# A graph network whose GpSimd gathers wait for TensorE: earlier TensorE steps for the attention's first chunks, and a last early chunk gathered in two halves

## The chip, the cores and the metric

The kernel runs on one core of one Trainium2 chip. The core has five engines with a queue of instructions each: TensorE (PE in the profile; its weight loads are PEld), VectorE (DVE), ScalarE (ACT), GpSimd (POOL) and SyncE (SP, which issues loads and stores here). 16 DMA engines move data between HBM and the core's memory. The metric is the time of one execution on the device, in microseconds (us); the figure for a kernel is the median of its timed runs.

## The reference: what is computed

One layer norm, then a graph network of two convolutions and one attention over 6250 nodes of 128 features and 200000 edges. The edges are sorted by their target node `dst`; `src` is random.

```python
h = max(layernorm(x), 0)
for (w1, b1, g, bt, w2, b2) in two convolutions:
    m   = concat(h[dst], h[src], edge_attr) @ w1 + b1
    m   = silu(group_norm(m, g, bt)) @ w2 + b2
    h   = segment_sum(m, dst) / count          # then a node's norm, silu, a residual
q, k, v = h @ qw + qb, h @ kw + kb, h @ vw + vb          # 8 heads of 16
logits  = (q[dst] * k[src]).sum(-1) * 16 ** -0.5 + edge_attr @ ew + eb
pe      = exp(logits - segment_max(logits, dst)[dst])
o       = segment_sum(pe / segment_sum(pe, dst)[dst] * v[src], dst)
out     = x + h + group_norm(o @ ow + ob)
```

## The kernel before

**Tiles and stages.** The nodes are cut into 49 tiles of 128. The edges are cut into 1563 columns of 128, and eight columns make a chunk (`TPC = 8`), so there are 196 chunks (`NCH`); chunk number `c` counts from the last edges backwards, and the last chunk, 195, has three columns. Three pipelines run over all chunks one after the other: convolution 1, convolution 2, attention. Between two of them the work of node tile 0 ends a layer (`last_tile`, lines 1188 to 1205): it can start only when the last chunk's sums are there.

**What an edge needs.** What comes from `dst` is read by SyncE as a window of consecutive rows (`pk`, from table `a_d`) and spread over the edges by a matmul with a one-hot matrix `ohT`, which ScalarE makes from a row of indices `rel` (lines 763 and 764; SyncE loads `rel` for two chunks at a time, line 725). What comes from `src` is gathered by GpSimd, a column at a time: line 796 is one indirect DMA of 128 rows, eight of them to a chunk (table `b_d` in the convolutions, `kv_d` in the attention). Besides 35 small one-hot instructions at the very end (line 1673) GpSimd does nothing else in the pipelines.

**Early chunks.** The next pipeline's first three chunks (`EARLY = 3`) are gathered before node tile 0 is done, from copies of the tables that lack it (`b_e`, `kv_e`). Tile 0's share, `late`, is then added by a matmul with a one-hot matrix `ohS` (line 1252 in convolution 2, `complete` with line 1700 in the attention). Chunk 3 is the first that is gathered from the whole table.

**Order.** The instructions of DVE, SP, ACT and PE stand in the order in which the program writes them, and each gather follows the gather before. Step `n` of `pipeline` (lines 893 to 957) issues the loads and the gathers of chunk `n + 2` (`ahead = 2`), then writes the work of chunk `n` and the products of chunk `n + 1`. In the attention a chunk's work is: `products` (line 1521, TensorE, into the one buffer `qe`), the product with the gathered keys (line 1536, DVE), a copy of the edge terms (line 1538, ACT; it frees `qe`), the head sums (line 1540). Chunks are collected in runs (chunks 0 to 3, then 4 to 11, then eight at a time); when a run is full its maxima are found (lines 1569 and 1570), and only then its chunks are weighted (line 1595, DVE), which frees their gather buffers, and summed (line 1602). The attention has 11 gather buffers (`ge0` to `ge2`, `g3` to `g9`, `gl`), the convolutions have four.

**The hold.** A gather waits for its buffer. Beside that, the first gather of a chunk is held until TensorE has come to a certain instruction:

```python
kept.seen = last_product() if fetched else None        # line 917, in pipeline, ahead of stage.fetch
if t == 0 and kept.seen is not None:                   # line 804, in gather
    held(h, kept.seen)
```

`last_product()` (line 810) is the TensorE instruction that was written last. In step `n` of the attention it is the end of the products of chunk `n`. The first chunk whose loads a pipeline issues inside its steps is not held (`fetched`): chunk 2 in convolution 1, chunk 3 in convolution 2, which finds its first three gathered, and chunk 2 in the attention, whose gathers are done by then, so that there chunk 3 is held. The early chunks, which the pipeline ahead gathers, are held in the same way (line 921); for chunk 2 of them this adds no wait, because GpSimd has waited for that TensorE instruction by then.

Of the kernel before, what the change touches and what calls it, by code (L numbers as in the profile page):

```python
# [31 lines left out]
TPC = 8  # L32
# [6 lines left out]
EARLY = 3  # L39
# [18 lines left out]
def kernel(ctx: ExitStack, tc: tile.TileContext, x, src, dst, eat, w, out):  # L58
# [12 lines left out]
    NCH = -(-EI // TPC)  # L71
# [16 lines left out]
    kept = SimpleNamespace(h0=hpc.tile([P, NW, D], FP, name="h0"))  # L88
# [80 lines left out]
    b_d = {i: dram.tile([NW * P, D], FP, name=f"b_d{i}") for i in (1, 2)}  # L169
    kv_d = dram.tile([NW * P, KV], FP, name="kv_d")  # L170
    b_e = dram.tile([NW * P, D], FP, name="b_e")
    kv_e = dram.tile([NW * P, KV], FP, name="kv_e")
# [72 lines left out]
    with tc.tile_pool(name="node0", bufs=1) as np_, tc.tile_pool(name="prep", bufs=1) as pp, \  # L245
# [99 lines left out]
        back, firsts = sums[:, :NCH], sums[:, 2 * P:2 * P + NCH]  # L345
# [445 lines left out]
            tc.add_to_no_dep_group(key, h.ins)  # L791

    def gather(k, g, table_d, ring=None):
        n = k.nt
        for t in range(n):
            h = nc.gpsimd.indirect_dma_start(  # L796
                out=g[:, t, :table_d.shape[1]], out_offset=None, in_=table_d,
                in_offset=bass.IndirectOffsetOnAxis(ap=k.src[:, t:t + 1], axis=0))
            if ring is None:
                continue  # L800
            if kept.behind is not None:
                follows(h, kept.behind)
            kept.behind = h.ins
            if t == 0 and kept.seen is not None:
                held(h, kept.seen)
            ring.mark(h, k.at, t, n - 1)

    kept.behind = kept.seen = None

    def last_product():  # L810
        return next((i.name for i in reversed(nc.cur_bb.bb.instructions) if i.engine == mybir.EngineType.PE), None)

    def held(h, name):
        tc.add_manual_dep(
            h.ins, name, mybir.DependencyInfo(mybir.DependencyClass.Sync, mybir.DependencyReason.DATA),
            reason="held until TensorE is there")
# [76 lines left out]
    def pipeline(i, stage, following=None, aside=iter(()), then=iter(())):  # L893


        ends, todo = steps_of(i)
        starts = {n: j for j, (n, _, _) in enumerate(plans[i])}
        ahead = stage.ahead
        ks, under_way, said, fetched = stage.ks, [], {}, False

        def go_on(n, those):
            for g in those:
                if said.get(g) == "held" and n + 1 in ends:
                    continue
                said[g] = next(g, STOP)
                if said[g] is STOP:
                    under_way.remove(g)

        for c in range(ahead):
            if c not in ks:  # L910
                ks[c] = stage.fetch(c)
                compared(ks[c])
        stage.products(ks[0])
        for n, seconds in enumerate(todo):
            new = None
            if n + ahead < NCH and n + ahead not in ks:
                kept.seen = last_product() if fetched else None
                new = ks[n + ahead] = stage.fetch(n + ahead)
                kept.seen, fetched = None, True
            elif following and n + ahead >= NCH:  # L920
                kept.seen = last_product()
                new = following.prefetch(n + ahead - NCH)
                kept.seen = None
            if n + 1 < NCH and stage.soon:
                stage.products(ks[n + 1])
            run = [ks[c] for c in ends.get(n, ())]
            stage.root(run)
            early = stage.soon and n > NCH - SOON
            if early:
                ahead_of = [g for g in under_way if said.get(g) not in ("var", "root")]  # L930
                go_on(n, ahead_of)
            if new and stage.soon:
                compared(new)
            first = (lambda k: lambda: stage.first(k))(ks[n]) if n < NCH else None
            stage.then = [ks[c] for c in (todo[n + 1] if n + 1 < len(todo) else ()) if c in ks]
            if stage.second(run, [ks.pop(c) for c in seconds], first) and first:
                first()
            stage.finish()
            if new and not stage.soon:
                compared(new)  # L940
            if n + 1 < NCH and not stage.soon:
                stage.products(ks[n + 1])
            if n + 1 < len(todo):
                stage.early(ks, n, todo[n + 1])
            if n in starts:
                for _ in aside:
                    pass
                under_way.append(stage.batch(starts[n]))
            go_on(n, [g for g in under_way if not early or g not in ahead_of])
            if n > 4 and next(aside, STOP) is STOP and n > min(starts):  # L950
                next(then, None)
            if n < NCH:
                stage.reduce(ks[n])
        stage.flush()
        for g in (*under_way, aside, then):
            for _ in g:
                pass
# [206 lines left out]
    def nodes_of(b, i, w, m, hx=None):  # L1164
        return attention_nodes(b, w, m, hx) if i == 3 else conv_nodes(b, i, w, m, last=hx is not None)
# [22 lines left out]
    def last_tile(b, i, hx=True):  # L1188

        slots, b.bank = b.bank(), None  # L1190
        turn = itertools.cycle(range(BN))

        def slot():
            j = next(turn)
            return slots[:, j:j + 1, :]

        b.bank = slot
        b.var = lambda: last_var
        b.rs = last_rs
        nc.scalar.activation(last_sd[:, :1], eps_t, AF.Sqrt)  # L1200
        for r in nodes_of(b, i, 0, 1, hx):
            if r == "root":
                nc.scalar.activation(last_sd, last_var, AF.Sqrt, bias=eps_t, scale=1.0 / HD)  # L1203
            if r == ("inverse" if i == 3 else "root"):
                nc.vector.reciprocal(last_rs, last_sd)  # L1205
# [10 lines left out]
    def convs(general=False):  # L1216
        with ExitStack() as es:
            pool = lambda n, b, **kw: es.enter_context(tc.tile_pool(name=f"{n}{'g' if general else 'c'}", bufs=b, **kw))
            pools = {"oh": pool("oh", 2), "ps": pool("ps", 1, space=PSUM)}
            if not general:  # L1220
                pools["ohT"] = pool("ohT", 2)
                ring = Ring("ring", GB)
# [75 lines left out]

            class Stage:
                ahead, soon = 2, True  # L1300

                def __init__(self, i):
                    self.i, self.ks = i, {}
# [10 lines left out]
                def fetch(self, c):  # L1314
                    k = chunk(self.i, c)
                    loads(k, self.pools, a_d[self.i], wc_d[self.i])
                    k.g = gp.tile([P, TPC, D], FP, name="g")
                    gather(k, k.g, b_d[self.i] if k.ohS is None else b_e, ring)
                    k.h = hs[c % len(hs)]
                    return k  # L1320

# [144 lines left out]
    gs = [None] * (G + 3)  # L1466

    class AheadOfAttention:

        @staticmethod  # L1470
        def prefetch(c):
            k = chunk(3, c)
            gather(k, gs[c], kv_e, ring3)

    ahead_of = AheadOfAttention()

    def attention(general=False):
# [197 lines left out]

        class Stage:
            ahead, soon = 2, False
            sums, late, nb = [], [], None
            lg, j, both = None, 0, None

# [257 lines left out]
```

## Time and profile before

| | |
|---|---|
| median of 3 runs | 6007.2 us (6005.33 to 6008.46) |
| the profiled execution | 6010.35 us, of which the span from the first to the last instruction is 6008.6 us |
| busy, as a share of the span | DVE 81%, POOL 75%, PE 61%, PEld 58%, ACT 55% |
| the last sums of convolution 1 and of convolution 2 start at | 2012.16 and 3970.94 us |

A row of the timeline gives start, duration, engine, line, operation, written and read tile, how many instructions it stands for, and in brackets the idle time of the engine ahead of it with what ended it. "issue" means that nothing in the profile's records was seen to release it. POOLq is the queue of GpSimd, which waits for semaphores ahead of the instructions. On POOL one gather is busy for 0.94 or 0.95 us and is followed by 0.30 us of idle time that belongs to it, so one takes 1.25 us and a chunk of eight 10.0 us.

### The profile page before, as it was taken

How to read it: one execution, taken by the hardware profiler on the slowest of the kernel's cores; microseconds unless marked ns; L12 is line 12 of the kernel's file. 1: busy time of each engine (PE TensorE's matmuls, PEld its weight loads, DVE VectorE, ACT ScalarE, POOL GpSimd, SP SyncE). 2: the span in 40 equal slices, each digit the busy share in tenths (PEclk: the TensorE clock that was granted, in tenths of full speed). 3: DMA queues.
4: the chain of work that ended last, by engine and by line, in shares of the span. 5: the costliest groups of instructions: out<-in, count | busy, mean ns of one | idle time of the engine just before them, and what ended most of it. 6: DMA issues, size and time to landing. Idle time of an engine off the chain costs nothing. (4 is left out here: it accounts for less than half of the span.)

```text
span 6008.6 us, 66534 instructions
## 1 busy us (share of the span) xinstructions
PE 3651.7 (61%) x20680; PEld 3461.7 (58%) x20681; DVE 4879.3 (81%) x6840; ACT 3324.6 (55%) x5207; POOL 4503.0 (75%) x4763
## 2 busy tenths in 40 slices
PE   6665555555555665555566655555666666666665
PEld 5555555555555555555555555555666565666565
DVE  7888888888888777777888888856787788888876
ACT  5666666666666666666666666642333333333574
POOL 7777777777777777777777777767777777777775
PEclk7667777777777777777777777867777777777777
DMA  5333333333333323233333333334444455555553
GB/s 158 90 108 100 80 87 89 91 92 89 91 92 88 81 78 81 78 82 78 83 98 99 100 98 102 102 86 137 137 135 136 135 140 144 142 147 138 147 143 84
DMA packets 384005, 640.81 MB, mean 107 GB/s; under 512 B 91184, under 2 KB 249628, under 8 KB 382059
## 3 DMA queue, kind: packets, MB, share of 16 engines
q0 software_dynamic: 175056, 410.03, 25.9%
q1 hardware_dynamic: 205482, 225.32, 13.1%
q8 instruction: 167, 2.74, 0.2%
q14 instruction: 196, 1.61, 0.1%
q10 hardware_dynamic: 3104, 1.12, 0.1%
HBM read 588.95 MB, written 47.17 MB: 106 GB/s over the span
## 5 line engine op out<-in xcount | busy, mean ns | idle before, releaser
L796 POOL DMA_INDIRECT g<-b_d,src_i x3102 | 2944.8, 949 | 951.6 <-issue 924.7
L1291 PE MATMUL u<-h,oh 128*128 128x129 f32 (+1 forms) x6252 | 1330.0, 399 | 1514.5 <-ACT h L1283 1514.5
L1291 PEld LDWEIGHTS u<-h,oh 128*128 128x128 f32 x6252 | 1229.3, 302 | 1590.9 <-ACT h L1283 1590.9
L796 POOL DMA_INDIRECT g<-kv_d,src_i x995 | 944.5, 949 | 333.9 <-issue 311.9
L1252 PE MATMUL m<-pk,ohT 101*128 101x128 f32 x6252 | 918.9, 309 | 63.7 <-DVE h L1259 44.3
L1252 PEld LDWEIGHTS m<-pk,ohT 101*128 101x128 f32 x6252 | 898.1, 228 | 75.7 <-DVE h L1259 53.7
L1259 DVE TENSOR_TENSOR h<-m,g 128x1024 f32<-128x1024 f32 x392 | 475.9, 1214 | 570.7 <-DMA g<-b_d,src_i 535.1
L1521 PE MATMUL qe<-pk,ohT 101*128 101x136 f32 x3126 | 595.6, 365 | 349.2 <-ACT ebs L1538 341.3
L1602 PE MATMUL us<-v,oh 128*128 128x145 f32 x3126 | 610.3, 366 | 294.1 <-DVE flat L1627 206.7
L1521 PEld LDWEIGHTS qe<-pk,ohT 101*128 101x128 f32 x3126 | 551.4, 263 | 383.9 <-ACT ebs L1538 375.5
L1602 PEld LDWEIGHTS us<-v,oh 128*128 128x128 f32 x3126 | 564.9, 256 | 337.4 <-DVE flat L1627 160.9
L1261 ACT ACTIVATE sq<-h 128x1024 f32<-128x1024 f32 x392 | 412.8, 1053 | 569.4 <-DVE h L1259 567.8
L1283 ACT ACTIVATE h<-h 128x1024 f32<-128x1024 f32 (+2 forms) x394 | 413.2, 1049 | 558.9 <-DVE h L1282 543.1
L763 ACT ACTIVATE ohT<-rel,minus_p 96x1024 f32<-96x1024 bf16 x588 | 668.7, 1137 | 16.8 <-DMA rel<-rel_d 8.6
L764 ACT ACTIVATE ohT<-ohT 96x1024 f32<-96x1024 f32 x588 | 619.9, 1054 | 19.2
L1263 DVE TENSOR_REDUCE var<-sq 128x64 f32<-128x1024 f32 x392 | 473.9, 1209 | 25.5 <-ACT sq L1261 25.1
L1281 DVE TENSOR_TENSOR h<-h,cps 128x1024 f32<-128x1024 f32 (+2 forms) x394 | 477.4, 1212 | 13.5
L1282 DVE TENSOR_TENSOR h<-h,cps 128x1024 f32<-128x1024 f32 (+2 forms) x394 | 477.4, 1212 | 13.5
L796 POOL DMA_INDIRECT ge<-kv_d,src_i x408 | 388.6, 952 | 124.3 <-issue 119.4
L1278 DVE TENSOR_TENSOR h<-h,cps 128x1024 f32<-128x1024 f32 (+2 forms) x394 | 474.5, 1204 | 0.8
L827 DVE TENSOR_TENSOR oh<-cps,dm 128x1024 f32<-128x1024 f32 x392 | 474.3, 1210 | 0.7 <-PE u L1291 0.6
L1615 ACT ACTIVATE us<-d 128x16 f32<-128x16 f32 x172 | 32.1, 187 | 602.6 <-DVE d L1611 435.2
(294 smaller groups left out, 4459.9 us busy)
## 6 DMA issues: line engine op xcount, KB each, us to landing
rel<-rel_d SPq DMA_DIRECT2D x291, 384.0 KB
g<-b_d,src_i POOLq DMA_INDIRECT x3102, 2.6
pk<-a_d SPq DMA_DIRECT2D x588, 46.0 KB
g<-kv_d,src_i POOLq DMA_INDIRECT x995, 2.8
ohT<-in_eat_dram SPq DMA_DIRECT2D x291, 40.0 KB
ge<-kv_d,src_i POOLq DMA_INDIRECT x408, 2.8
a_d<-n_o SPq DMA_DIRECT2D x24, 256.0 KB
kv_d<-n_o SPq DMA_DIRECT2D x24, 256.0 KB
```

The source lines that it names most:

```text
L763: nc.scalar.activation(k.ohT[:WN, :], k.rel, AF.Square, bias=minus_p[:WN])
L764: nc.scalar.activation(k.ohT[:WN, :], k.ohT[:WN, :], AF.Relu, bias=1.0, scale=-4.0)
L796: h = nc.gpsimd.indirect_dma_start(out=g[:, t, :table_d.shape[1]], out_offset=None, in_=table_d, in_offset=bass.IndirectOffsetOnAxis(ap=k. ...
L827: return nc.vector.tensor_tensor(k.oh[:, :k.nt, :], iota[:, None, :].to_broadcast([P, k.nt, P]), k.dm[:, :, None].to_broadcast([P, k.nt, P ...
L1252: nc.tensor.matmul(k.m[:, t, :], lhsT=lhs[:, t * P:(t + 1) * P], rhs=rhs, start=(j == 0), stop=(j == len(terms) - 1))
L1259: nc.vector.tensor_tensor(k.mt, k.m[:, :n], k.g[:, :n], ALU.add)
L1278: nc.vector.tensor_tensor(m4, m4, k.rs.rearrange("p (t g) -> p t g", g=H)[:, a:a + n, :, None].to_broadcast([P, n, H, HD]), ALU.mult)
L1281: nc.vector.tensor_tensor(mt, mt, over_edges(gam, n), ALU.mult)
L1282: nc.vector.tensor_tensor(mt, mt, over_edges(bet, n), ALU.add)
L1291: nc.tensor.matmul(k.u[:, 0, :wide(k)], lhsT=k.oh[:, t, :], rhs=k.h[:, t, :wide(k)], start=start and t == 0, stop=stop and t == k.nt - 1)
L1521: nc.tensor.matmul(k.qe[:, t // TB, at:at + DB], lhsT=lhs[:, t * P:(t + 1) * P], rhs=rhs, start=(j == 0), stop=(j == len(terms) - 1))
L1602: nc.tensor.matmul(k.u[:, :wide], lhsT=k.oh[:, t, :], rhs=k.v[:, t, :wide], start=(t == 0), stop=(t == k.nt - 1))
```

## The change

Three things are changed, all of them in what GpSimd's gathers wait for.

First, in each pipeline the step notes TensorE's last instruction in a list (`marks`), and a chunk's first gather is held by the mark of the step `lag(c)` steps back, not by the latest. In the convolutions `lag` is 0. In the attention it is 3 for chunks up to 11, 2 for 12 and 13, 1 for 14 to 18 and for the last chunk, and 0 for all others. No hold at all is set up to chunk 3 (`n + ahead > EARLY`), nor where the step would lie ahead of the first one, as for chunk 4 of the attention.

Second, the last of the three early chunks, chunk 2, is written in two halves of four columns. The first half is written, and so held, after the last step's work, by the last sums of the pipeline that ends; the second half inside node tile 0's work (`last_tile`, at its seventh step, `n == 6`), held by that tile's latest TensorE instruction. Before, all eight were written at once, with a hold that added no wait.

Third, a hold is used up by the gather that takes it (`kept.seen = None`).

```diff
--- before.py
+++ after.py
@@ -791,8 +791,16 @@
             tc.add_to_no_dep_group(key, h.ins)
 
     def gather(k, g, table_d, ring=None):
+        for _ in gathered(k, g, table_d, ring):
+            pass
+
+    def gathered(k, g, table_d, ring, halves=False):
+
         n = k.nt
         for t in range(n):
+            if halves and t % (TPC // 2) == 0:
+                yield
+                kept.seen = last_product()
             h = nc.gpsimd.indirect_dma_start(
                 out=g[:, t, :table_d.shape[1]], out_offset=None, in_=table_d,
                 in_offset=bass.IndirectOffsetOnAxis(ap=k.src[:, t:t + 1], axis=0))
@@ -801,11 +809,17 @@
             if kept.behind is not None:
                 follows(h, kept.behind)
             kept.behind = h.ins
-            if t == 0 and kept.seen is not None:
+            if (t == 0 or halves) and kept.seen is not None:
                 held(h, kept.seen)
+                kept.seen = None
             ring.mark(h, k.at, t, n - 1)
-
-    kept.behind = kept.seen = None
+        yield
+
+    def early_gather(c, *what):
+        kept.rest = gathered(*what, c == EARLY - 1)
+        next(kept.rest)
+
+    kept.behind = kept.seen = kept.rest = None
 
     def last_product():
         return next((i.name for i in reversed(nc.cur_bb.bb.instructions) if i.engine == mybir.EngineType.PE), None)
@@ -896,7 +910,7 @@
         ends, todo = steps_of(i)
         starts = {n: j for j, (n, _, _) in enumerate(plans[i])}
         ahead = stage.ahead
-        ks, under_way, said, fetched = stage.ks, [], {}, False
+        ks, under_way, said, marks = stage.ks, [], {}, []
 
         def go_on(n, those):
             for g in those:
@@ -913,10 +927,12 @@
         stage.products(ks[0])
         for n, seconds in enumerate(todo):
             new = None
+            marks.append(last_product())
             if n + ahead < NCH and n + ahead not in ks:
-                kept.seen = last_product() if fetched else None
+                back = n - stage.lag(n + ahead)
+                kept.seen = marks[back] if n + ahead > EARLY and back >= 0 else None
                 new = ks[n + ahead] = stage.fetch(n + ahead)
-                kept.seen, fetched = None, True
+                kept.seen = None
             elif following and n + ahead >= NCH:
                 kept.seen = last_product()
                 new = following.prefetch(n + ahead - NCH)
@@ -951,6 +967,8 @@
                 next(then, None)
             if n < NCH:
                 stage.reduce(ks[n])
+        if following:
+            next(kept.rest)
         stage.flush()
         for g in (*under_way, aside, then):
             for _ in g:
@@ -1198,7 +1216,9 @@
         b.var = lambda: last_var
         b.rs = last_rs
         nc.scalar.activation(last_sd[:, :1], eps_t, AF.Sqrt)
-        for r in nodes_of(b, i, 0, 1, hx):
+        for n, r in enumerate(nodes_of(b, i, 0, 1, hx)):
+            if i < 3 and n == 6:
+                next(kept.rest)
             if r == "root":
                 nc.scalar.activation(last_sd, last_var, AF.Sqrt, bias=eps_t, scale=1.0 / HD)
             if r == ("inverse" if i == 3 else "root"):
@@ -1298,6 +1318,7 @@
 
             class Stage:
                 ahead, soon = 2, True
+                lag = staticmethod(lambda c: 0)
 
                 def __init__(self, i):
                     self.i, self.ks = i, {}
@@ -1315,7 +1336,10 @@
                     k = chunk(self.i, c)
                     loads(k, self.pools, a_d[self.i], wc_d[self.i])
                     k.g = gp.tile([P, TPC, D], FP, name="g")
-                    gather(k, k.g, b_d[self.i] if k.ohS is None else b_e, ring)
+                    if k.ohS is None:
+                        gather(k, k.g, b_d[self.i], ring)
+                    else:
+                        early_gather(c, k, k.g, b_e, ring)
                     k.h = hs[c % len(hs)]
                     return k
 
@@ -1470,7 +1494,7 @@
         @staticmethod
         def prefetch(c):
             k = chunk(3, c)
-            gather(k, gs[c], kv_e, ring3)
+            early_gather(c, k, gs[c], kv_e, ring3)
 
     ahead_of = AheadOfAttention()
 
@@ -1675,6 +1699,7 @@
 
         class Stage:
             ahead, soon = 2, False
+            lag = staticmethod(lambda c: 3 if c < 12 else 2 if c < 14 else 1 if c < 19 or c == NCH - 1 else 0)
             sums, late, nb = [], [], None
             lg, j, both = None, 0, None
 
```

No instruction moves on any engine; what changes is which semaphores the gathers wait for. Two places of POOL show it. `ge` with a number is a buffer of an early chunk, `g` with a number the buffer of a later chunk, `ring3` a count of landed gathers, DMAHW the stores and loads that SP issued, PE TensorE's count.

The first place is the seam from convolution 2 to the attention, chunk 2 (table `kv_e`) and the first gather of chunk 3 (table `kv_d`). Before:

```order
L796 DMA ge_5561<-kv_e,src_i 128x256
L796 DMA ge_5561<-kv_e,src_i 128x256 [waits ring3_r1]
L796 DMA ge_5561<-kv_e,src_i 128x256 [waits ring3_r2]
L796 DMA ge_5561<-kv_e,src_i 128x256 [waits ring3_r3]
L796 DMA ge_5561<-kv_e,src_i 128x256 [waits ring3_r4]
L796 DMA ge_5561<-kv_e,src_i 128x256 [waits ring3_r5]
L796 DMA ge_5561<-kv_e,src_i 128x256 [waits ring3_r6]
L796 DMA ge_5561<-kv_e,src_i 128x256
L796 DMA g_22588<-kv_d,src_i 128x256 [waits DMAHW3_49,DMAHW5_49,DMAHW1_49,DMAHW6_49,DMAHW0_49,DMAHW7_49,PE_49,Pool_49]
```

And now:

```order
L804 DMA ge_5561<-kv_e,src_i 128x256 [waits PE_49]
L804 DMA ge_5561<-kv_e,src_i 128x256 [waits ring3_r1]
L804 DMA ge_5561<-kv_e,src_i 128x256 [waits ring3_r2]
L804 DMA ge_5561<-kv_e,src_i 128x256 [waits ring3_r3]
L804 DMA ge_5561<-kv_e,src_i 128x256 [waits PE_49,ring3_r4]
L804 DMA ge_5561<-kv_e,src_i 128x256 [waits ring3_r5]
L804 DMA ge_5561<-kv_e,src_i 128x256 [waits ring3_r6]
L804 DMA ge_5561<-kv_e,src_i 128x256
L804 DMA g_22588<-kv_d,src_i 128x256 [waits DMAHW5_49,DMAHW3_49,DMAHW6_49,DMAHW1_49,DMAHW7_49,DMAHW0_49,Pool_49]
```

The first and the fifth gather of chunk 2 have gained a wait for TensorE, and the first of chunk 3 has lost one; its waits for stores of `kv_d` stay.

The second place follows: the last gather of chunk 3, chunk 4, and the first gather of chunk 5. Before:

```order
L796 DMA g_22588<-kv_d,src_i 128x256
L796 DMA g_22589<-kv_d,src_i 128x256 [waits PE_49]
L796 DMA g_22589<-kv_d,src_i 128x256 [waits ring3_r1]
L796 DMA g_22589<-kv_d,src_i 128x256 [waits ring3_r2]
L796 DMA g_22589<-kv_d,src_i 128x256 [waits ring3_r3]
L796 DMA g_22589<-kv_d,src_i 128x256 [waits ring3_r4]
L796 DMA g_22589<-kv_d,src_i 128x256 [waits ring3_r5]
L796 DMA g_22589<-kv_d,src_i 128x256 [waits ring3_r6]
L796 DMA g_22589<-kv_d,src_i 128x256 [waits DMASW4_49]
L796 DMA g_22590<-kv_d,src_i 128x256 [waits DVE_49,PE_49,Activation_49]
```

And now:

```order
L804 DMA g_22588<-kv_d,src_i 128x256
L804 DMA g_22589<-kv_d,src_i 128x256
L804 DMA g_22589<-kv_d,src_i 128x256 [waits ring3_r1]
L804 DMA g_22589<-kv_d,src_i 128x256 [waits ring3_r2]
L804 DMA g_22589<-kv_d,src_i 128x256 [waits ring3_r3]
L804 DMA g_22589<-kv_d,src_i 128x256 [waits ring3_r4]
L804 DMA g_22589<-kv_d,src_i 128x256 [waits ring3_r5]
L804 DMA g_22589<-kv_d,src_i 128x256 [waits ring3_r6]
L804 DMA g_22589<-kv_d,src_i 128x256 [waits DMASW4_49]
L804 DMA g_22590<-kv_d,src_i 128x256 [waits DVE_49,PE_49,Activation_49]
```

Chunk 4 waits for nothing of TensorE any more. Chunk 5 and later ones show the same names, but the count of TensorE that they wait for is a lower one: for chunk 5 the products of chunk 0, before those of chunk 3.

The same happens at two more places of POOL: at the seam from convolution 1 to convolution 2 (table `b_e`) chunk 2 gains the two waits, and in convolution 1 chunk 3 loses its wait for TensorE. The last chunk of the attention loses its wait for TensorE too, and the one-hots after it take one on.

## The prediction

> **What bounds the kernel now.** I read the busy time per engine first, then the totals of the waits, then GpSimd's timeline. First the page's engines and its two largest rows of gathers, then three rows of the totals of waits (total, times, longest):
>
> ```profile
> PE 3651.7 (61%) x20680; PEld 3461.7 (58%) x20681; DVE 4879.3 (81%) x6840; ACT 3324.6 (55%) x5207; POOL 4503.0 (75%) x4763
> L796 POOL DMA_INDIRECT g<-b_d,src_i x3102 | 2944.8, 949 | 951.6 <-issue 924.7
> L796 POOL DMA_INDIRECT g<-kv_d,src_i x995 | 944.5, 949 | 333.9 <-issue 311.9
> POOL g L796 <- issue: 1243.9, 4002, 20.8
> DVE h L1259 <- DMA g<-b_d,src_i: 535.1, 257, 8.3
> DVE g L1536 <- DMA g<-kv_d,src_i: 133.5, 62, 6.9
> ```
>
> VectorE is the busiest, but it waits hundreds of times for gathered data. POOL's 75% is not slack: a gather is busy 0.949 us, and 924.7 / 3102 = 0.30 us of idle time belong to each, so at 1.25 us each the stream is full. A hole in it delays the data of all that follows; where VectorE still waits for a gather after the hole, the hole is in the time. The rows to find are idle times over 0.30 us. At the seam to the attention, GpSimd's timeline:
>
> ```profile
> 3985.97 0.95 POOL L796 DMA_INDIRECT ge<-kv_e,src_i  x1 [0.30 <-issue]
> 3989.72 0.95 POOL L796 DMA_INDIRECT ge<-kv_e,src_i  x1 [0.30 <-issue]
> 4011.50 0.94 POOL L796 DMA_INDIRECT g<-kv_d,src_i  x1 [20.84 <-issue]
> ...
> 4024.36 0.94 POOL L796 DMA_INDIRECT g<-kv_d,src_i  x1 [3.16 <-PE qe L1521]
> ...
> 4038.15 0.94 POOL L796 DMA_INDIRECT g<-kv_d,src_i  x1 [4.09 <-issue]
> 4039.40 0.95 POOL L796 DMA_INDIRECT g<-kv_d,src_i  x1 [0.30 <-issue]
> ...
> 5949.05 0.94 POOL L796 DMA_INDIRECT g<-kv_d,src_i  x1 [3.90 <-PE qe L1521]
> ```
>
> These are the first gathers of chunks 3, 4, 5 and, last, 195; from 4039.40 to 5949.05 each gather follows its predecessor within about 0.30 us. The 20.84 and the 4.09 name no releaser. TensorE's attention products, chunks 0 to 3 (and 8, for later), do:
>
> ```profile
> 3993.67 4.00 PE L1521 MATMUL qe<-pk,ohT 101*128 101x136 f32 x16 [7.75 <-ACT ohT L764]
> 4006.74 4.00 PE L1521 MATMUL qe<-pk,ohT 101*128 101x136 f32 x16 [3.00 <-ACT ebs L1538]
> 4020.09 4.00 PE L1521 MATMUL qe<-pk,ohT 101*128 101x136 f32 x16 [3.00 <-ACT ebs L1538]
> 4033.60 3.79 PE L1521 MATMUL qe<-pk,ohT 101*128 101x136 f32 x16 [3.00 <-ACT ebs L1538]
> ...
> 4071.49 3.99 PE L1521 MATMUL qe<-pk,ohT 101*128 101x136 f32 x16 [2.47 <-ACT ebs L1538]
> ```
>
> Products of chunk 1 end at 4010.74, of chunk 2 at 4024.09, of chunk 3 at 4037.39; the gathers start 0.76, 0.27 and 0.76 us after. So the three holes are the holds. GpSimd's queue (durations min/median/max of two waits, first and last start) and SyncE's issues say when the other waits of chunk 3 were over:
>
> ```profile
> L796 POOLq EVENT_SEMAPHORE  x2: 5203/14704/24205, 3981.3 to 3986.6; - x2
> 3983.06 1.56 SPq L1080 DMA_DIRECT2D kv_d<-late  x2
> 3987.22 0.33 SPq L725 DMA_DIRECT2D rel<-rel_d  x1
> 3994.68 0.31 SPq L725 DMA_DIRECT2D rel<-rel_d  x1
> ```
>
> The queue waited 5.2 us to 3986.5, for the last stores of `kv_d`, then 24.2 us from 3986.6 to 4010.8, which is the end of chunk 1's products. Without the hold chunk 3 may follow chunk 2 at once.
>
> **The change part by part.**
>
> *Chunk 3 of the attention, hold gone.* Chunk 2's last gather starts at 3989.72, the next may at 3990.97, 4.5 us after the stores. 4011.50 − 3990.97 = 20.53 us. The bounds: 20.53, if the stores are all that is left to wait for, and 0, if something unseen holds it too. I take 20.53, as the queue's row ends with TensorE.
>
> *Chunk 4, hold gone:* 3.16 − 0.30 = 2.86 us. *Chunk 5, now held by chunk 0's products* (3997.67), wanted at 4010.97: 4.09 − 0.30 = 3.79 us. Its other two waits name work of node tile 0, which ends ahead of the attention.
>
> *Chunks 6 to 18, earlier holds.* Chunk 6 would start at 4020.97, each later one 10.0 us on. Chunks 6, 7 and 8 wait for the products of chunks 1, 2 and 3. Closest is chunk 8: wanted at 4040.97, released at about 4037.39 + 0.76 = 4038.15, 2.8 us to spare. Cost 0, bounded by 2.8 us of delay in the early products.
>
> *Convolution 1, chunk 3, hold gone:*
>
> ```profile
> 72.69 0.94 POOL L796 DMA_INDIRECT g<-b_d,src_i  x1 [1.05 <-PE m L1252]
> ```
>
> 1.05 − 0.30 = 0.75 us, early in a stream that stays full; bounds 0 and 0.75, and I take 0.75.
>
> *Chunk 2 in halves: two new waits at each seam.* At both seams, the ends of the last sums (line 1291) and of the transpose of node tile 0 that the fifth gather waits for (line 972); then the first and fifth gathers at seam 1 (at seam 2 the fifth is the 3985.97 above):
>
> ```profile
> 2012.16 4.79 PE L1291 MATMUL u<-h,oh 128*128 128x129 f32 x22 [6.91 <-ACT h L1283]
> 2021.35 0.47 PE L972 MATMUL nd<-ident,n_A 128*128 128x128 f32 x1 [2.00 <-DVE n_A L1001]
> 2022.79 0.94 POOL L796 DMA_INDIRECT g<-b_e,src_i  x1 [0.30 <-issue]
> 2027.78 0.94 POOL L796 DMA_INDIRECT g<-b_e,src_i  x1 [0.30 <-issue]
> 3970.94 5.00 PE L1291 MATMUL u<-h,oh 128*128 128x128 f32 x22 [7.22 <-ACT h L1283]
> 3979.90 0.47 PE L972 MATMUL nd<-ident,n_A 128*128 128x128 f32 x1 [1.23 <-DVE n_A L1001]
> 3980.97 0.95 POOL L796 DMA_INDIRECT ge<-kv_e,src_i  x1 [0.30 <-issue]
> ```
>
> Margins at seam 1: 2022.79 − 2016.95 = 5.8 and 2027.78 − 2021.82 = 6.0 us; at seam 2: 3980.97 − 3975.94 = 5.0 and 3985.97 − 3980.37 = 5.6 us. Behind a gather that waits, the whole stream waits, so past the margin each microsecond would be a microsecond of the kernel. With the 0.75 us from convolution 1, the margins stay above 4. Cost 0.
>
> *The last chunk's hold, one step earlier.* It frees 3.90 − 0.30 = 3.6 us, on three gathers. The last data that VectorE waits for in the attention:
>
> ```profile
> 5796.05 1.29 DVE L1536 TENSOR_TENSOR g<-qe,g 128x768 f32<-128x768 f32 x2 [1.48 <-DMA g<-kv_d,src_i]
> ```
>
> From there to the end the compute is the limit, so this is worth between 0 and 3.6 us, and I take 0.
>
> *Does the gain reach the end?* A stream 27.2 us earlier helps only where data are late. VectorE's key products of chunks 7, 8 and 12, and the weighting that frees buffer `g4`:
>
> ```profile
> 4069.79 1.29 DVE L1536 TENSOR_TENSOR g<-qe,g 128x768 f32<-128x768 f32 x2 [1.01 <-DMA g<-kv_d,src_i]
> 4079.96 1.29 DVE L1536 TENSOR_TENSOR g<-qe,g 128x768 f32<-128x768 f32 x2 [3.69 <-DMA g<-kv_d,src_i]
> ...
> 4119.81 1.29 DVE L1536 TENSOR_TENSOR ge<-qe,ge 128x768 f32<-128x768 f32 x2 [7.20 <-DMA ge<-kv_d,src_i]
> 4130.13 1.22 DVE L1595 TENSOR_TENSOR v<-g,pe 128x1024 f32<-128x1024 f32 x1 [0.38 <-ACT v L1591]
> ```
>
> Chunk 7 is the first that waits. Without waits, a chunk here takes what lies between chunk 7's key products and the end of chunk 8's products: 4075.48 − 4069.79 = 5.7 us, against 10 between arrivals. From 4068.78, chunk 12 is reached at 4068.78 + 5 × 5.7 = 4097.3, 22.5 us earlier; the other 5 us come in at the waits that follow. Chunk 4's weighting would end 10.3 + 1.2 us after that, at 4108.8, and chunk 15's gathers into its buffer are wanted at 4110.97: 2.1 us to spare. From then on stream and compute are as they were, earlier by the whole shift, until 5796, and so is the compute-bound rest.
>
> **The sum:** 0.75 + 20.53 + 2.86 + 3.79 = 27.9 us. The profiled execution took 6010.35 us, 1.7 us beyond its span and 3.2 us above the median of 6007.2; it would take 6010.35 − 27.9 = 5982.4. From the median I forecast 5979.3 us.
>
> **A rule against it.** The moved gathers now run beside the attention's first loads. ScalarE at its first two one-hot matrices, and the stretch that POOL idled through (busy PE, PEld, DVE, ACT, POOL with counts, clock, share of the DMA engines, GB/s):
>
> ```profile
> 3991.38 1.15 ACT L763 ACTIVATE ohT<-rel,minus_p 96x1024 f32<-96x1024 bf16 x1 [5.15 <-DMA rel<-rel_d]
> 4006.62 1.15 ACT L763 ACTIVATE ohT<-rel,minus_p 96x1024 f32<-96x1024 bf16 x1
> 3991.00:4011.50 20.50, 13.52 (x51) 11.92 (x52) 5.18 (x6) 6.71 (x8) 0.00 (x0) 0.67 0.15 46
> ```
>
> The load of `rel` issued at 3987.22 landed by 3991.38, 4.16 us later, with chunk 2's gathers running. The next, issued at 3994.68, is used at 4006.62: even at twice 4.16 us it lands at 4003.0, in time. The DMA engines' share in the stretch was 0.15. So the sum stays 27.9 us. The Trainium skill, "DMA: Bandwidth & Descriptors", section "Issuing engines are not separate DMA queues", says that transfers started by different engines run on the same 16 DMA engines and interleave; by that rule the first loads would be slower beside gathers. The 4.16 us fit it, as they already hold such company, and the sum by it would be the same while the loads stay below 12 us.
>
> **The rivals.**
>
> *Part of the gain is lost at a buffer or a hold* (chunk 15's buffer with 2.1 us, chunk 8's hold with 2.8). With gathers beside them the attention's first seven chunks may run slower by d; POOL then waits d − 2.1 at chunk 15. For it: in the long hole the compute ran with no gathers beside it. Against it: chunks 3 to 6 did have them, and their products ran as fast or faster (3.79 after 4.00). With d of 5 to 12 us it gives 3 to 10 us back: 5982 to 5989.
>
> *Chunk 3 does not move*, because something unseen releases it. Then 0.75 + 2.86 + 3.79 = 7.4 us are left: 5999.8. For it: the row says "issue". Against it: the queue's 24.2 us end with the products.
>
> *Slower.* The first rival's mechanism, stronger: the slowing d eats the whole shift at 27.9 + 2.1 = 30 us and makes the kernel slower by over 12 us from d = 42, 6 us on each of the first seven chunks, half of the 13 us from one product to the next. At d = 45 it gives 6007.2 + 15 = 6022. Nothing in the rows comes near it.
>
> *The tail gains too*, since the last chunk's 3.6 us count: 5975.7.
>
> **How the numbers follow.** A measurement of this kernel tells a change from none at about 0.2%, 12 us. The forecast, 5977 to 5982: 0.68. Part lost, 5982 to 5990: 0.15. The tail too: 0.05. All three are faster: 0.88. Chunk 3 unmoved or most of the gain lost, 5995 to 6019: 0.07. Slower: 0.05. The range from 5975, the tail's case, to 5990, the end of the part lost, leaves out 0.12.
>
> **What would show it.** Right: POOL's idle time ahead of chunk 3 is 0.30 to 1 us and its first gather stands 10.0 us after chunk 2's first, near 3990; ahead of chunks 4 to 18 and at both seams no idle time over 0.5 us; VectorE's wait at chunk 12 falls from 7.20 to under 1 us; the last wait for a gather comes near 5768. Wrong: an idle time of microseconds at chunk 2 of a seam, at chunk 8 or at chunk 15, or a wait of POOL's queue that ends with a store; and if the attention's first seven chunks take over 2 us longer, the shift is cut there. If the last wait moves but the end does not, the stretch after 5796 has a limit of its own.

## The result, and the profile after

The changed kernel takes 5976.6 us (median of 5 runs, 5975.6 to 5978.0); the kernel before took 6007.3 us on the same chip (5 runs, 6005.3 to 6008.9). That is 30.7 us less, a ratio of 0.995 with a 95% interval from 0.9937 to 0.9963, or 22 to 38 us. The forecast was 5979.3 us, 27.9 us less.

The page of the profile after, engines and the two rows of gathers, then the totals of waits:

```profile
PE 3628.6 (61%) x20680; PEld 3434.9 (57%) x20681; DVE 4878.0 (82%) x6840; ACT 3323.7 (56%) x5207; POOL 4500.5 (75%) x4763
L804 POOL DMA_INDIRECT g<-b_d,src_i x3102 | 2942.6, 949 | 951.0 <-issue 922.6
L804 POOL DMA_INDIRECT g<-kv_d,src_i x995 | 944.5, 949 | 303.1 <-issue 285.1
POOL g L804 <- issue: 1215.1, 3969, 5.9
```

Work and counts are the same; what has gone is idle time ahead of the attention's gathers, 333.9 − 303.1 = 30.8 us. GpSimd's timeline at the seam to the attention, at chunk 15 and at the last chunk:

```profile
3985.88 0.95 POOL L804 DMA_INDIRECT ge<-kv_e,src_i  x1 [0.30 <-issue]
3987.13 0.95 POOL L804 DMA_INDIRECT g<-kv_d,src_i  x1 [0.30 <-issue]
...
4107.08 0.95 POOL L804 DMA_INDIRECT g<-kv_d,src_i  x1 [0.30 <-issue]
...
5913.99 0.95 POOL L804 DMA_INDIRECT g<-kv_d,src_i  x1 [0.30 <-DVE v L1619]
```

Chunk 3 follows chunk 2 at once. From there to the last gather no gather waits longer than its 0.3 us. VectorE's key products of chunks 8, 11 and 12, the weighting that frees chunk 15's buffer, and the last wait for a gather (line 1560 is the old 1536, 1619 the old 1595):

```profile
4071.45 1.29 DVE L1560 TENSOR_TENSOR g<-qe,g 128x768 f32<-128x768 f32 x2
...
4086.06 1.29 DVE L1560 TENSOR_TENSOR ge<-qe,ge 128x768 f32<-128x768 f32 x2 [2.86 <-PE qe L1545]
4091.70 1.29 DVE L1560 TENSOR_TENSOR ge<-qe,ge 128x768 f32<-128x768 f32 x2 [2.77 <-PE qe L1545]
4102.02 1.22 DVE L1619 TENSOR_TENSOR v<-g,pe 128x1024 f32<-128x1024 f32 x1 [0.37 <-ACT v L1615]
...
5764.65 1.29 DVE L1560 TENSOR_TENSOR g<-qe,g 128x768 f32<-128x768 f32 x2 [1.37 <-DMA g<-kv_d,src_i]
```

Where VectorE waited about 7 us for gathers, it waits 2.8 us for TensorE: the compute catches up at its own pace. The buffer of chunk 15 is free at 4103.24, 3.8 us before it is wanted. The last wait for a gather stands 31.4 us earlier.

The start of the same gather in both profiled executions, after less before, worked out gather by gather:

| gather | shift, us | step |
|---|---|---|
| first of all | −0.94 | ahead of everything that changed |
| convolution 1, chunk 3 | −2.02 | −0.75 at this hold, −0.33 ahead of it |
| last of chunk 2 at the seam to the attention | −3.84 | −1.8 net, in steps of 0.2 to 0.5 both ways over 3900 us |
| attention, chunk 3 | −24.37 | −20.5 |
| chunk 4 | −27.25 | −2.9 |
| chunk 5 | −31.06 | −3.8 |
| seven eighths through the attention | −30.95 | |
| the end of the span | −34.8 | |

The three steps at the seam are the three terms, to 0.1 us. The rest of the −34.8 us is in no term: −3.1 us of small steps before the seam, and −3.8 us behind it, nearly all of them in the compute-bound tail (experiment 3 comes back to these). The profiled execution of before was 3 us above its median, that of after 1 us below, so the pair of profiles lies 4 us further apart than the medians.

### The profile page after: what moved, and what is told of

The parts are those of the page before. It is cut to its first block, busy times and chain, and to the rows that moved or that the text cites. A ratio compares the mean times of both kernels' runs of the same rounds, so it can differ in the third digit from the quotient of the medians.

```text
span 5973.8 us, 66535 instructions
## 1 busy us (share of the span) xinstructions
PE 3628.6 (61%) x20680; PEld 3434.9 (57%) x20681; DVE 4878.0 (82%) x6840; ACT 3323.7 (56%) x5207; POOL 4500.5 (75%) x4763
## 3 DMA queue, kind: packets, MB, share of 16 engines
q10 hardware_dynamic: 3104, 1.12, 0.1%
## 5 line engine op out<-in xcount | busy, mean ns | idle before, releaser
L804 POOL DMA_INDIRECT g<-kv_d,src_i x995 | 944.5, 949 | 303.1 <-issue 285.1
```

Of the source, the lines that this page charges most:

```text
L804: h = nc.gpsimd.indirect_dma_start(out=g[:, t, :table_d.shape[1]], out_offset=None, in_=table_d, in_offset=bass.IndirectOffsetOnAxis(ap=k. ...
```

## The experiments

The experiments ran on four chips, and on two of them the kernel before takes 7040 and 6972 us instead of 6004 and 6018, so each time stands beside the kernel before on the same chip. The kernel before was profiled only for the result above, so its rows come from there. Each diff is against the changed kernel.

**1. The halves alone.** All holds as in the kernel before, so that the halves of chunk 2 are the only change from it.

```diff
-            lag = staticmethod(lambda c: 3 if c < 12 else 2 if c < 14 else 1 if c < 19 or c == NCH - 1 else 0)
+            lag = staticmethod(lambda c: 0)
-                kept.seen = marks[back] if n + ahead > EARLY and back >= 0 else None
+                kept.seen = marks[back] if n + ahead > EARLY or (n + ahead == EARLY and i != 2) else None
```

> The kernel before with the halves of chunk 2 alone: all other holds as before. Theory: the two new waits at each seam end 4 to 6 us before the gathers are due, so nothing changes: within 1.5 us of the kernel before. Rival (the halves bring the 2.8 us by which the changed kernel is faster than forecast): 3 us faster.

6005.0 us against 6004.2, a ratio of 1.0001 (0.9992 to 1.001). So the halves neither cost nor bring anything that can be told, within about 6 us either way, and in the trace no gather of chunk 2 waits beyond its 0.3 us at either seam. In the profiled execution the holes of before are back, and the hold in convolution 1 shows a size that the profile of before did not:

```profile
73.24 0.94 POOL L804 DMA_INDIRECT g<-b_d,src_i  x1 [2.93 <-PE m L1272]
4013.92 0.94 POOL L804 DMA_INDIRECT g<-kv_d,src_i  x1 [21.89 <-issue]
4026.49 0.94 POOL L804 DMA_INDIRECT g<-kv_d,src_i  x1 [2.87 <-PE qe L1545]
4040.34 0.94 POOL L804 DMA_INDIRECT g<-kv_d,src_i  x1 [4.15 <-issue]
```

Chunk 3 of convolution 1 waits 2.93 us, where it waited 1.05.

**2. The changed kernel without the halves.**

```diff
-        kept.rest = gathered(*what, c == EARLY - 1)
+        kept.rest = gathered(*what)
```

(Not shown: the two calls `next(kept.rest)` become `next(kept.rest, None)`.)

> The changed kernel without the halves: chunk 2 is gathered as before, with a hold that adds no wait. Theory: within 1.5 us of the changed kernel. Rival: 3 us slower than it.

5977.3 us against 6004.2 of before, 26.9 us less (0.9942 to 0.9969). So the gain is in the holds that were moved or dropped, as far as the runs can tell; this and experiment 1 say so from both sides.

**3. The last chunk's hold as before.**

```diff
-            lag = staticmethod(lambda c: 3 if c < 12 else 2 if c < 14 else 1 if c < 19 or c == NCH - 1 else 0)
+            lag = staticmethod(lambda c: 3 if c < 12 else 2 if c < 14 else 1 if c < 19 else 0)
```

> The changed kernel with the last chunk held by the latest TensorE step, as before; nothing else differs. Theory: the gathers of the last chunk start 3 to 4 us later and the end does not move: within 1.5 us of the changed kernel. Rival (the tail gains from the earlier hold): 3.3 us slower than the changed kernel.

```profile
5918.24 0.94 POOL L804 DMA_INDIRECT g<-kv_d,src_i  x1 [1.89 <-PE qe L1545]
```

The hole ahead of the last chunk is back, 1.6 us of it, and the time is 5977.4 us against 5977.3 in experiment 2, the nearest kernel on that chip, whose runs lie 5 us apart. The trace says more: beside the profile after, VectorE's scans stand 2.7 to 3.3 us later ahead of this hole and 2.9 to 3.0 behind it, so it does not add to the end. The tail's hold is worth nothing that can be told, as costed. The 3.8 us that the first pair of profiles shows behind the seam come from elsewhere. VectorE's scan of the maxima near the tail's start, before:

```profile
5803.83 2.29 DVE L1569 TENSOR_TENSOR_SCAN blk<-nbs,blk 40x1024 f32<-40x1024 bf16 x1 [1.18 <-PE blk L1565]
```

and the same scan after:

```profile
5771.28 2.28 DVE L1593 TENSOR_TENSOR_SCAN blk<-nbs,blk 40x1024 f32<-40x1024 bf16 x1
```

The wait of 1.18 us for TensorE's transposes is not there in the second execution; the shift grows from 31.3 to 32.6 us at this scan, and by less than 1.1 us each at later ones. The change does not decide it. The profile of experiment 2, with all holds moved, has the wait:

```profile
5775.52 2.29 DVE L1593 TENSOR_TENSOR_SCAN blk<-nbs,blk 40x1024 f32<-40x1024 bf16 x1 [1.05 <-PE blk L1589]
```

So have those of experiments 1 and 4 (1.12 and 1.25 us); those of this experiment and of the second runs of experiments 5 and 7 have not.

**4. A hold put back in the convolutions.** The changed kernel, with chunk 3 held in both convolutions.

```diff
-                kept.seen = marks[back] if n + ahead > EARLY and back >= 0 else None
+                kept.seen = marks[back] if n + ahead >= EARLY and back >= 0 else None
```

> The changed kernel with chunk 3 held again in the two convolutions, by the products of chunk 1; the attention is unchanged. Theory (in the convolutions too a hole in the stream of gathers goes into the time at its full length): in convolution 2 chunk 3 was gathered from 2029.9 and the products of chunk 1 end at about 2035.3, so a hole of 5.5 to 6.2 us appears there and one of 0.7 in convolution 1; 6 to 7 us slower than the changed kernel. Rival (VectorE is the bound there and covers it): within 1.5 us of it.

```profile
72.16 0.94 POOL L804 DMA_INDIRECT g<-b_d,src_i  x1 [1.71 <-PE m L1272]
...
2032.87 0.94 POOL L804 DMA_INDIRECT g<-b_d,src_i  x1 [1.19 <-DVE var L1283]
```

The holes are 1.4 us and 0.9 us, not 0.7 and 5.5 to 6.2: I had counted chunk 2's products, which follow chunk 1's without a gap, as chunk 1's. (The second row names VectorE; TensorE's products of chunk 1 end at 2032.60, 0.27 us ahead of the gather.) Beside the profile of experiment 3, the shift of the same gather is 1.2 us behind the first hole, 2.4 behind the second, and 2.0 in the middle of the attention, 3000 us on. Beside that of experiment 2 it is 1.1, 2.2 and 1.1. So half of the holes or more stays in the stream; small steps at other places, up to 0.8 us, which any two profiles show, hide whether all of it does. The time is 5983.1 us (5979.9 to 5985.9), 5.8 above experiments 2 and 3; holes of 2.3 us are not 5.8, and the agreement with the number expected is luck, as the holes came out otherwise. Of the 4.1 us by which this profiled execution is longer than that of experiment 3, over 2 come in the tail, with the wait named there. The rival's "within 1.5 us" is not what was seen, but the size is open.

**5. Only chunk 3 is free.** The changed kernel with a lag of 0 everywhere.

```diff
-            lag = staticmethod(lambda c: 3 if c < 12 else 2 if c < 14 else 1 if c < 19 or c == NCH - 1 else 0)
+            lag = staticmethod(lambda c: 0)
```

> As the changed kernel, but every hold of the attention from chunk 4 on names the latest TensorE step again; only chunk 3 is free. Theory (the last hold that binds sets the stream): chunk 3 is gathered 20.5 us earlier, but chunk 4 still waits for the products of chunk 2 and chunk 5 for those of chunk 3, so that chunk 5 starts where it did before; nothing of the 27.2 us is gained at this seam, and the time is 0.7 us under the kernel before (convolution 1), about 6006. Rival (each idle time is a cost of its own, as the sum of the prediction has it): 20.5 + 0.7 us are gained, 5986.

It ran where the kernel before takes 7039.8 us: 7023.2 us, a ratio of 0.9975 (0.9964 to 0.9987), 16.5 us less. Run again on a chip where before takes 6018.3 us:

> The same kernel as lag0, for a comparison with the kernel before at about 6005 us: the first one was measured where TensorE itself waited for work that the profile doesn't name and the kernel before took 7039.8 us. Every hold of the attention from chunk 4 on names the latest TensorE step again; only chunk 3 is free. Theory (the last hold that binds sets the stream): the idle time ahead of chunk 3 is gone, but the idle times ahead of chunks 4 and 5 grow by as much, chunk 5 starts where it did, and the time is within 1.5 us of 0.7 us under the kernel before. Rival (each idle time is a cost of its own): 21 us faster than before.

6011.8 us, 6.5 us less, a ratio of 0.9994 (0.9985 to 1.0004): no change that can be told, and not the 21 us. On the chip of 7039.8 us the theory missed: 16.5 us, with an interval of 9 to 25, leaves out the 0.7 expected and holds the rival's 21. GpSimd's timeline shows that the holds act in the same way on both chips. First that second run, from chunk 2's last gather on, with TensorE's products of chunks 1 to 3:

```profile
3989.32 0.94 POOL L804 DMA_INDIRECT ge<-kv_e,src_i  x1 [0.30 <-issue]
3990.57 0.95 POOL L804 DMA_INDIRECT g<-kv_d,src_i  x1 [0.30 <-issue]
4017.99 0.94 POOL L804 DMA_INDIRECT g<-kv_d,src_i  x1 [17.73 <-PE qe L1545]
4028.64 0.94 POOL L804 DMA_INDIRECT g<-kv_d,src_i  x1 [0.90 <-issue]
4005.45 2.12 PE L1545 MATMUL qe<-pk,ohT 101*128 101x136 f32 x16 [3.00 <-ACT ebs L1562]
4015.59 2.12 PE L1545 MATMUL qe<-pk,ohT 101*128 101x136 f32 x16 [2.99 <-ACT ebs L1562]
4025.75 2.12 PE L1545 MATMUL qe<-pk,ohT 101*128 101x136 f32 x16 [3.00 <-ACT ebs L1562]
```

Then the first run, on the other chip:

```profile
4689.66 0.94 POOL L804 DMA_INDIRECT g<-kv_d,src_i  x1 [26.98 <-PE qe L1545]
4703.44 0.95 POOL L804 DMA_INDIRECT g<-kv_d,src_i  x1 [4.07 <-issue]
4698.88 3.79 PE L1545 MATMUL qe<-pk,ohT 101*128 101x136 f32 x16 [3.00 <-issue]
```

The hole of 20.84 us ahead of chunk 3 is gone, and a hole of 17.73 or 26.98 us stands ahead of chunk 4. Chunk 5 starts with the end of chunk 3's products, as before. At this seam the next holds take back what freeing chunk 3 alone gives. Where the 16.5 us come from on the chip of 7040 us is open, as the kernel before was not profiled there. That chip is a poor place for the question, because the stream of gathers isn't full there, as this gather of convolution 1 shows:

```profile
336.33 0.94 POOL L804 DMA_INDIRECT g<-b_d,src_i  x1 [3.45 <-remote]
```

"remote" too means that the profile doesn't see who released it. In the profile of the first run 366 gathers wait over 0.6 us, 364 of them the first of a chunk, in all three pipelines, 1039 us in all beyond the 0.30 us of each; the execution is 1045 us longer than the profiled one of after. In the second run's profile only three gathers behind the very first wait that long, all in the attention.

The second run shows one more thing. Each set of 16 products took 2.12 us, where the profile of before has 4.00 and 3.79, so chunk 3's products ended 38.6 us after chunk 2's last gather, not 47.7. This execution took 5997.5 us, the shortest of its ten (to 6021.0). So the length of the holes depends on how fast TensorE runs just then.

**6. One and two steps back.** The lag of 3 cut to 1, and to 2.

```diff
-            lag = staticmethod(lambda c: 3 if c < 12 else 2 if c < 14 else 1 if c < 19 or c == NCH - 1 else 0)
+            lag = staticmethod(lambda c: 1 if c < 19 or c == NCH - 1 else 0)
```

and, for two, `2 if c < 14 else 1 if c < 19 or c == NCH - 1 else 0`.

> As the changed kernel, with a lag of 1 where it has 3 or 2. Theory: chunk 6 is the one that waits for the products of chunk 3 (about 4038.2 in the trace before), and chunk 6 stood at 4048.2 before; the gain at the seam is 10.0 us, in all 10.7, and the time is about 17 us above the changed kernel. Rival (each idle time by itself): all three holes are gone or shortened, 27 us, as the changed kernel.

> As the changed kernel, with a lag of 2 where it has 3. Theory: chunk 7 waits for the products of chunk 3, at about 4038.2, and stood at 4058.2 before; the gain at the seam is 20.0 us, in all 20.7, and the time is about 7 us above the changed kernel. Rival: as the changed kernel.

7028.5 and 7019.8 us against 7039.8. With 16.5 us less for a lag of 0, 11.3 for 1 and 19.9 for 2, and runs that lie 15 to 28 us apart, the times there give no order. The profiles say what became of the step from lag 0 to lag 1. With a lag of 1 chunk 8 starts 9.2 us earlier than with 0, at 4727.16, but then chunk 15 waits for its buffer, and chunk 19, the first with a lag of 0 again, for TensorE:

```profile
4814.19 0.94 POOL L804 DMA_INDIRECT g<-kv_d,src_i  x1 [7.56 <-DVE v L1619]
4868.49 0.94 POOL L804 DMA_INDIRECT g<-kv_d,src_i  x1 [11.39 <-PE qe L1545]
```

Chunk 19 starts 4.0 us later than with a lag of 0. Both were run again, and again on a chip of that kind (before 6971.7 us):

> The same kernel as lag1, for a comparison where TensorE doesn't starve. The attention's holds name the TensorE step one back. Theory (the last hold that binds sets the stream): chunk 6 waits for the products of chunk 3 and starts at about 4038 us of the trace before where it stood at 4048.2; 10.7 us faster than the kernel before, 17 slower than the changed kernel. Rival (each idle time is a cost of its own): 27 us faster.

> The same kernel as lag2, likewise, with the holds two steps back. Theory: chunk 7 waits for the products of chunk 3 and starts at about 4038 us where it stood at 4058.2; 20.7 us faster than the kernel before, 7 slower than the changed kernel. Rival: 27 us faster.

6963.0 us (0.9984 to 1.0003) and 6954.0 us (0.9967 to 0.9985): 8.6 and 17.6 us less, where 10.7 and 20.7 were expected. The first interval, −2 to 11 us, holds the 10.7 and no change at all; the second, 10 to 23 us, holds the 20.7; the rival's 27 us lie outside both. Here too some 360 gathers wait over 0.6 us. In the two profiles the last step is 9.6 us at chunk 15, 10.2 at chunk 100 and 2.8 at chunk 190, so the times don't measure it well. The positions at the seam are those expected. One step back, first gathers of chunks 4 to 6, and the end of the products of chunk 3:

```profile
4616.87 0.94 POOL L804 DMA_INDIRECT g<-kv_d,src_i  x1 [11.06 <-PE qe L1545]
4629.39 0.94 POOL L804 DMA_INDIRECT g<-kv_d,src_i  x1 [2.83 <-issue]
4641.94 0.95 POOL L804 DMA_INDIRECT g<-kv_d,src_i  x1 [2.86 <-PE qe L1545]
4637.68 4.00 PE L1545 MATMUL qe<-pk,ohT 101*128 101x136 f32 x16 [3.00 <-ACT ebs L1562]
```

Two steps back, chunks 4, 5 and 7, and the products of chunk 3:

```profile
4608.21 0.95 POOL L804 DMA_INDIRECT g<-kv_d,src_i  x1 [1.78 <-PE qe L1545]
4620.30 0.95 POOL L804 DMA_INDIRECT g<-kv_d,src_i  x1 [2.39 <-issue]
4649.12 0.94 POOL L804 DMA_INDIRECT g<-kv_d,src_i  x1 [9.08 <-PE qe L1545]
4644.85 4.00 PE L1545 MATMUL qe<-pk,ohT 101*128 101x136 f32 x16 [4.89 <-ACT ebs L1562]
```

Each step of lag moves the wait for chunk 3's products one chunk on: to chunk 5 at lag 0, chunk 6 at lag 1 (4641.94 after 4641.68), chunk 7 at lag 2 (4649.12 after 4648.85). A chunk is 10 us of stream, so each step is worth up to 10 us, until at lag 3 chunk 8 wants its data later than those products end.

**7. No holds in the attention.**

```diff
-            lag = staticmethod(lambda c: 3 if c < 12 else 2 if c < 14 else 1 if c < 19 or c == NCH - 1 else 0)
+            lag = staticmethod(lambda c: NCH)
```

> As the changed kernel, with no hold in the attention but those of the early chunks. Theory: with the lag of 3 no hold binds any more, so the time is that of the changed kernel within 1.5 us, and no gather of the attention waits over 0.5 us. Rival (the holds that are left still cost, or they keep the gathers out of the way of the first loads): some us faster, or some us slower with the products of chunks 0 to 7 taking longer than 69 us from first to last.

> The same kernel as free, likewise. Theory: no hold binds in the changed kernel, so without them the time is the changed kernel's, 28 to 31 us under the kernel before, on a chip where TensorE doesn't starve. Rival (gathers that run as far ahead as the 11 buffers let them take something from TensorE or from the loads on any chip): slower than the kernel before, as in the first run of it, where it took 434 us more; then the holds of the changed kernel from chunk 19 on earn their place here too.

On the chip of before's 6018.3 us it takes 5990.5 us: 27.8 us less (0.9935 to 0.9968), about what the changed kernel gains elsewhere, which was not run on that chip. No hold that the change left costs anything that can be told there. Where before takes 7039.8 us, it takes 7474.0 us: 434 us more (ratio 1.0604, 1.0585 to 1.0623). VectorE at the attention's start there:

```profile
4675.76 1.22 DVE L1727 TENSOR_TENSOR ge<-ge,blk 128x1024 f32<-128x1024 f32 x1 [24.45 <-remote]
4694.71 1.22 DVE L1727 TENSOR_TENSOR ge<-ge,blk 128x1024 f32<-128x1024 f32 x1 [17.74 <-remote]
4731.20 1.22 DVE L1727 TENSOR_TENSOR ge<-ge,blk 128x1024 f32<-128x1024 f32 x1 [32.36 <-remote]
```

Beside gathers that run without a stop for seven chunks, the attention's first chunks stall there for 17 to 32 us at a time. What they wait for can't be read from the trace, and whether the gathers cause it isn't shown. Nor is the loss only there: against the kernel with a lag of 0 on the same chip, the same gather is 42 us later at chunk 25, 222 at chunk 100 and 402 at the last chunk. The changed kernel itself was not run on such a chip; with two steps back, gathers ran without a stop for two chunks at most, and the kernel was 19.9 us faster than before there and 17.6 on the chip of 6972 us.

## Why the prediction was right

**The three terms at the seam** (20.53, 2.86, 3.79 us) came out as 20.5, 2.9 and 3.8. Reading the 20.84 us as the TensorE hold, though the row says "issue", was right: without the hold the gather starts at once, and the rival that something unseen releases it falls.

**That the gain reaches the end** was right, with the margins on the cautious side: chunk 15's buffer had 3.8 us to spare, not 2.1, since the first compute-bound chunks took 6.4, 3.9, 5.0, 5.7 and 5.6 us where 5.7 was put for each. One sign was missed: VectorE's wait at chunk 12 was to fall from 7.20 to under 1 us, and is 2.77. It is for TensorE and no longer for a gather, and lies inside the 5.6 us that the chunk takes, so it costs nothing beyond the pace that was put. **The early compute** was not slowed by the gathers that now run beside it, on this chip: the products of chunks 0 to 7 start 68.8 us apart from first to last, before 69.2. The rivals "part lost" and "slower" rested on such a slowing. The first load of `rel`, issued at 3983.67, is used by ScalarE at 3988.14, 4.5 us later, before 4.2; in experiment 1, where gathers stop ahead of chunk 3 as before, it is 5.2, so this is no slowing that the moved gathers can be blamed for. The second load is used at 4003.11 without a wait. The rule of the Trainium skill, "DMA: Bandwidth & Descriptors", section "Issuing engines are not separate DMA queues", is neither borne out nor contradicted by these loads; what it would cost stayed inside their margin, as forecast.

**The zeros**, for the halves (experiments 1 and 2), for the later holds (7) and for the last chunk (3), are zeros within what the runs can tell; and in the trace after, no gather but the very first has more than 0.32 us of idle time ahead of it.

**What was mis-sized** is convolution 1's chunk 3: 0.75 us in the profile of before, 2.6 and 1.4 us in other executions with that hold. So the forecast of 27.9 us was drawn from one execution of a time that varies: the four comparisons without binding holds at the seam gave 30.7, 26.9, 26.8 and 27.8 us. What the 30.7 us hold beyond 27.9 is inside the interval, and its cause is not settled.

**What the sum hid** is that its terms don't stand by themselves. They could be added because all three holds go in the same edit; as a list of prices they mislead: with chunk 3 alone freed, chunk 5 starts with the end of chunk 3's products as before, and on the chip of 6018 us no gain can be told (experiment 5). What counts is the last hold that binds and where its chunk would stand without it.

## What to carry to other kernels

An engine that shows 75% busy can be the bound: look for the idle time that belongs to each instruction, and then for what exceeds it. Where several waits stand one behind another on such an engine, don't price each by its idle time; take the last one that binds, and ask when the work behind it could start if all were gone. A wait that ties a saturated stream to another engine's progress also takes over that engine's speed and its scatter.

## What was not expected

- **With the holds the time scattered more.** On the chip of 6004 us the kernel before lay between 5996.1 and 6011.3 us in 15 runs, and with the halves alone between 5997.4 and 6011.7; without the binding holds the same chip gave 5976.5 to 5981.6 and 5975.9 to 5979.7, in five runs each. The five runs of before for the result above lay within 3.6 us, so few runs need not show it. That the holds pass on TensorE's scatter is argued, not shown: the 16 products on whose end the holds waited take 4.00 us in the profiles of before and of experiment 1, long executions of 6010 and 6012 us, and 2.12 in that of experiment 5's second run, the shortest of its ten. The Trainium skill, "TensorE: Matmul & The Clock Gate", section "Part 1: The HAM clock gate (the "warmup" mystery)", has two clocks, a half and a full one, and a warm-up whose phase varies from run to run; 4.00 / 2.12 = 1.9 agrees, and so does the way of the granted clocks, 0.75 in the profile of before and 0.84 in experiment 5's, in the 80 us after the seam.
- **The same holds may be worth something on another chip.** With none in the attention the kernel is 6% slower than before where that takes 7040 us, and 27.8 us faster where it takes 6018. Why those two chips are slower, and whether the gathers take something there, is open.
